# Graph layer with residual norm on one core: the order and the engines of the last split's steps

## The chip, the cores and the metric

One core of one Trainium2 chip runs the kernel. Its time is device microseconds for one execution; the median of 3 runs of the kernel before is 1138.0 us (1137.83 to 1139.56). The profile is of one further execution, whose own numbers stand in a table below. Engines are named as in the profile: PE multiplies matrices and writes PSUM, DVE (VectorE), ACT (ScalarE) and POOL (GpSimd) work element by element, and SP issues most transfers. Each engine works through its own queue in order, so an instruction that waits holds up everything behind it on that engine.

## What is computed

100,000 edges join 6,250 nodes. For each edge the rows of its two nodes and its own row of 128 attributes are multiplied by a 384x128 weight, normalised, scaled and cut at zero. The results are summed by source node, added to the node's own row x, and normalised again:

```
msg_in = jnp.concatenate([x[row], x[col], edge_attr], axis=-1)
h = msg_in @ W + b
h = (h - mu) * jax.lax.rsqrt(var + LN_EPS) * gamma + beta
out = jax.ops.segment_sum(jax.nn.relu(h), row, num_segments=N)
x = _layernorm(x + out, axis=-1)
```

`row` is an edge's source `src`, `col` its target `dst`; edges come sorted by target. The kernel checks the ranges of its inputs and falls back to a general path when they don't fit, which is not run here.

## The kernel before

**Two passes.** Edges come in 782 tiles of 128. The first pass multiplies the attributes and the target rows of four tiles at a time (`edges`, L531 and L535), evicts them (`evict`, L543) and scatters every row to memory, sorted by the block of its source node (`scatters`, L561: one indirect transfer of POOL per tile). There are 50 blocks of 125 nodes. The second pass loads the sorted rows block by block, two blocks (a **pair**) at a time, and needs all scatters of the rows that it loads. The tiles are therefore cut into six **splits** (`SPLITS`): while split s is multiplied and scattered, the pairs of split s-1 are worked through. The last split has 78 tiles, and nothing follows it. Its 25 pairs of 4 tiles, with the finishing of the 50 blocks, are the **tail** (`tail`, L962 to L1001), which starts when the last scatter has landed.

**The steps of a pair** (`class Pair`). `load_pair` (L614, SP) brings the rows `hl`, with the node's number within its block in column D. `ones` (L632, DVE) makes the one-hot matrix `ohe` of all four tiles in one instruction. `turn` (L644, PE) transposes it, `turned` (L648, ACT) copies it to `ohn` as bf16. `pick` multiplies `ohn` with the projected node rows `xa`, twelve matmuls (L671), onto a PSUM bank that was seeded with `hl`. In the tail the seed is a matmul of `hl` with the identity (L665, in `pick`); the banks are called `sel` for even and `hp` for odd pairs. `square` squares and sums the four tiles on ACT (L680) and takes the root (L683), `root` the reciprocal on DVE (L689), `scale` writes the four scaled and cut messages on DVE (L695), `sums` adds them up per node on PE (L704, bank `pa`, of which there is one), and `add` adds that to `acc` on DVE (L712).

**The finishing of two blocks** (`class Finish`). `begin` loads two blocks of x (L725, SP) and forms y from `acc` and x with two instructions of POOL (L728, L729). `stats` adds the shift and the total on DVE (L735, two). `root` squares on ACT (L745, two) and takes a root of its own (L748). `norm` and `moved` (L753, L758, DVE) give scale and shift, `end` applies them with two instructions of POOL (L764, L765; the last two blocks on ACT, L768) and stores (L770, SP).

**The order.** Inside `manual_schedule` PE, DVE, ACT and SP run in the order in which the program calls the steps; POOL's order is left to the scheduler. `work(n)` advances the pairs of the older splits by `FLOW`. Behind the last scatters the old pairs still have steps left. The program calls `tail(-2)` and `tail(-1)`, with the first two one-hots and the first transposition of the last split, between those steps, and then `tail(0)` to `tail(30)`. In `tail(i)` DVE does the reciprocal of pair i-1, the one-hot of i+2, the messages of i-1, the finishing's total of i-3, its reciprocal and shift of i-4, and the addition of i-1; PE does seed and pick of i, the transposition of i+1 and the sums of i-1; ACT does squares and root of finishing i-4, the copy of `ohn` of i+1, squares and root of pair i; POOL has in the built kernel, in turn, L764 and L765 of one block pair and L728 and L729 of the one three later.

Of the kernel before, what the change touches and what calls it, by code (L numbers as in the profile page):

```python
# [50 lines left out]
XG = 4  # L51
ROW = 132
# [31 lines left out]
def fast_path(ctx, tc, io, bad_d):  # L84
# [533 lines left out]
    class Pair:  # L618
# [8 lines left out]
        def ones(self):  # L627

            blk, k = late["blk"], self.k
            self.hl = loaded.pop((self.s, self.p))  # L630
            self.ohe = blk.tile([P, KMAX, P], F32, name="ohe", bufs=4)
            nc.vector.tensor_tensor(self.ohe[:, :k, :],  # L632
                                    self.hl[:, :k, D:D + 1].to_broadcast([P, k, P]),
                                    row_bc(iota_p, k), op=ALU.is_equal)
# [20 lines left out]

        def pick(self, g):
# [3 lines left out]
            if g in self.sel:  # L660
                sel = self.sel[g]
            else:
                name = "hp" if (g + self.p * len(self.groups)) % 2 else "sel"
                sel = psum.tile([P, PT, P], F32, name=name, bufs=BANKS[name])
                nc.tensor.matmul(sel[:, :m, :], ident, self.hl[:, j0:j0 + m, 0:D], start=True,  # L665
                                 stop=False, skip_group_check=True)
                self.sel[g] = sel
            for j in range(m):
                b = 2 * self.p + (j0 + j) % 2
                for i in range(3):  # L670
                    pe(nc.tensor.matmul(sel[:, j, :], self.ohn[:, j0 + j, :],  # L671
                                        xa[:, b, i * D:(i + 1) * D], start=False,
                                        stop=j == m - 1 and i == 2, skip_group_check=True))

# [41 lines left out]
    class Finish:  # L716
# [5 lines left out]
        def begin(self):  # L722
            fin, b0, n = late["fin"], self.b0, self.n
            xs = fin.tile([P, FN, D], F32, name="xs", bufs=3)
            nc.sync.dma_start(flat(xs), io["xblk"][:, b0 * D:(b0 + n) * D])  # L725
            self.y = fin.tile([P, FN, D], F32, name="y", bufs=6)
            engine = nc.gpsimd if b0 + n < NB else nc.vector
            engine.tensor_tensor(self.y, acc[:, b0:b0 + n, 0:D], row_bc(g2, n), op=ALU.mult)  # L728
            engine.tensor_tensor(self.y, self.y, xs, op=ALU.add)  # L729

        def stats(self):
            fin, y = late["fin"], self.y
            total = fin.tile([P, FN], F32, name="total", bufs=4)
            for j in range(self.n):
                nc.vector.scalar_tensor_tensor(y[:, j, :], beta_p, acc[:, self.b0 + j, D:D + 1],  # L735
                                               y[:, j, :], op0=ALU.mult, op1=ALU.add,
                                               accum_out=total[:, j:j + 1])
            self.total = total

        def root(self):  # L740
            fin = late["fin"]
            fsq = fin.tile([P, FN, D], F32, name="fsq")
            var = fin.tile([P, FN], F32, name="var")
# [212 lines left out]
    def at(p):  # L956
        return 0 <= p < n
# [311 lines left out]
```

## Time and profile before

| | us |
|---|---|
| median of 3 runs | 1138.0 |
| the profiled execution's own time | 1138.6 |
| its span, first to last instruction | 1136.7 |
| mean granted clock of PE in it | 0.894 |
| PE, DVE, ACT, POOL busy in the span | 859.8, 882.7, 735.6, 837.0 |
| last scatter issued | 1033.08 |
| first one-hot of the last split starts | 1037.87 |
| first and last pick of the last split start | 1043.09, 1118.72 |
| last write of the result on an engine ends | 1129.76 |

A row of a timeline gives the start, the length, the engine, the line, and in brackets how long the engine stood idle before it and what ended that. "x4" are four instructions shown as one. A length is that of the instruction; the next one of the same engine can start before it is over, so the cost of an instruction on its engine is the distance to the next start.

### The profile page before, as it was taken

The numbers are of one execution on the slowest core, as the hardware profiler recorded it, in microseconds if no ns is written. First come the engines' busy times: TensorE is split into PE (matmuls) and PEld (weight loads), VectorE is DVE, ScalarE is ACT, GpSimd is POOL, SyncE is SP. The second block draws the span as 40 slices with busy tenths as digits, with TensorE's granted clock in tenths as the row PEclk, the third lists the DMA queues.
The fourth block names the chain that finished last, engine by engine and source line by source line (L and its number), as shares of the span: only waits on it lengthen the run. The fifth ranks groups of instructions, "written<-read, shape, count | busy, mean of one in ns | idle before, by whom it ended". The sixth has DMA issues, their size and how long they took to land.

```text
span 1136.7 us, 27306 instructions
## 1 busy us (share of the span) xinstructions
PE 859.8 (76%) x8671; PEld 798.3 (70%) x8671; DVE 882.7 (78%) x2444; ACT 735.6 (65%) x3104; POOL 837.0 (74%) x899
## 2 busy tenths in 40 slices
PE   3657755445877878787778878898989899986994
PEld 2546644345877778686777877888988898975673
DVE  7987776326878777778677778988999987875996
ACT  1334332115666676576766777887988999994996
POOL 2777777777777777777777777777777777773786
PEclk9878786657989989899889999998999999998998
DMA  6799996438877756677777749776877677742562
GB/s 198 230 282 280 292 288 203 140 105 263 252 243 241 246 179 190 216 241 243 226 244 225 229 125 316 253 251 205 279 249 237 209 230 221 237 140 88 159 171 83
DMA packets 126674, 247.47 MB, mean 218 GB/s; under 512 B 47356, under 2 KB 61197, under 8 KB 126519
## 3 DMA queue, kind: packets, MB, share of 16 engines
q1 hardware_dynamic: 100356, 191.52, 56.2%
q0 software_dynamic: 25184, 53.31, 13.2%
q8 instruction: 70, 1.15, 0.4%
q10 hardware_dynamic: 978, 0.80, 0.3%
q14 instruction: 86, 0.70, 0.2%
HBM read 155.74 MB, written 89.80 MB: 216 GB/s over the span
## 4 chain that ended last, share of the span: by engine, by line
PE 29%; DMA 24%; DVE 24%; ACT 11%; issue 7%; POOL 2%; SPq 1%; ACTq 0%; POOLq 0%; DVEq 0%
DMA sorted<-hs,place_i 18%; PE pa L704 9%; DVE msg L695 7%; PE hp L531 7%; PE sel L671 6%; DMA db<-drel_d 4%; ACT sq L680 3%; DVE ohe L632 3%; DVE sc L391 3%; PE beside L428 2%; ACT sel L654 2%; POOL sorted L561 2%; ACT hs L543 2%; ACT ohn L648 2%; PE tr L644 2%
## 5 line engine op out<-in xcount | busy, mean ns | idle before, releaser
L561 POOL DMA_INDIRECT sorted<-hs,place_i x782 | 771.0, 986 | 240.9 <-issue 98.8
L704 PE MATMUL pa<-msg,ohe 128*128 128x130 f32 x1900 | 268.1, 292 | 23.3 <-DVE acc L712 15.3
L531 PE MATMUL hp<-w,eT 128*128 128x128 f32 x1564 | 248.2, 309 | 49.2 <-ACT hs L543 44.3
L543 ACT COPY hs<-hp 128x512 f32<-128x512 f32 x196 | 114.0, 582 | 258.7 <-DMA sorted<-hs,place_i 193.3
L671 PE MATMUL sel<-xa,ohn 128*128 128x128 bf16 x2706 | 198.7, 225 | 106.3 <-ACT sel L654 105.5
L671 PEld LDWEIGHTS <-ohn 128*128 128x128 bf16 x2850 | 182.9, 100 | 133.5 <-issue 112.6
L704 PEld LDWEIGHTS pa<-msg,ohe 128*128 128x128 f32 x1900 | 240.3, 201 | 34.3 <-DVE acc L712 18.7
L695 DVE SCALAR_TENSOR_TENSOR msg<-sel,rstd,cut 128x128 f32<-128x128 f32 x902 | 255.2, 345 | 8.0
L531 PEld LDWEIGHTS hp<-w,eT 128*128 128x128 f32 x1564 | 221.2, 218 | 54.6 <-ACT hs L543 48.8
L680 ACT ACTIVATE sq<-sel 128x128 f32<-128x128 f32 x902 | 238.1, 282 | 17.4 <-PE sel L671 16.7
L680 ACT ACTIVATION_READ_ACCUMULATOR sq<-sel 128x1 f32 x902 | 191.6, 212 | 0.0
L632 DVE TENSOR_TENSOR ohe<-hl,beside 128x1024 f32<-128x1024 f32 (+2 forms) x150 | 147.9, 986 | 37.4 <-DMA hl<-sorted 30.9
L654 ACT COPY sel<-hl 128x512 f32<-128x512 f32 (+1 forms) x225 | 127.9, 568 | 19.4 <-DVE msg L695 19.1
L648 ACT COPY ohn<-tr 128x1024 bf16<-128x1024 bf16 (+2 forms) x150 | 123.7, 825 | 18.4 <-PE tr L644 18.2
L689 DVE RECIPROCAL rstd<-std 128x4 f32<-128x4 f32 (+1 forms) x250 | 42.9, 172 | 84.7 <-ACT std L683 83.8
L519 DVE TENSOR_SCALAR ohd<-db,part_w 128x512 bf16<-128x512 bf16 x194 | 71.8, 370 | 46.7 <-DMA db<-drel_d 25.2
L644 PE MATMUL tr<-ident_h,ohe 128*128 128x128 bf16 x950 | 81.6, 226 | 10.5 <-issue 7.2
L535 PE MATMUL hp<-win,ohd 126*128 126x128 bf16 x782 | 83.3, 233 | 4.1 <-DVE ohd L519 3.5
L683 ACT ACTIVATE std<-ss,eps 128x4 f32<-128x4 f32 (+1 forms) x250 | 74.3, 297 | 8.1
L535 PEld LDWEIGHTS <-ohd 126*128 126x128 bf16 x782 | 66.9, 106 | 8.7 <-DVE ohd L519 3.7
L712 DVE TENSOR_TENSOR acc<-acc,pa 128x260 f32<-128x260 f32 x125 | 52.3, 418 | 26.4 <-PE pa L704 26.3
L644 PEld LDWEIGHTS <-ohe 128*128 128x128 bf16 x950 | 63.8, 102 | 11.8 <-issue 7.7
(159 smaller groups left out, 807.6 us busy)
## 6 DMA issues: line engine op xcount, KB each, us to landing
eT<-in_eT SPq DMA_DIRECT2D x96, 512.0 KB
hl<-sorted SPq DMA_DIRECT2D x75, 528.0 KB
db<-drel_d SPq DMA_DIRECT2D x96, 256.0 KB
sorted<-empty SPq DMA_DIRECT2D x100, 198.0 KB
hl<-sorted SPq DMA_DIRECT2D x50, 264.0 KB
sorted<-hs,place_i POOLq DMA_INDIRECT x782
hl<-sorted SPq DMA_DIRECT2D x25, 396.0 KB
sorted<-empty SPq DMA_DIRECT2D x50, 132.0 KB
```

The costliest lines, as they stand in the source:

```text
L531: pe(nc.tensor.matmul(hp[:, j, :], eT[:, at], w[:, 2, :], start=j == 0, stop=False, skip_group_check=True), 4)
L535: pe(nc.tensor.matmul(hp[:, j, :], oh[:3 * WN, at], win[:3 * WN, :], start=False, stop=j == m - 1, skip_group_check=True))
L543: nc.scalar.copy(hs[:, :m, 0:D], hp[:, :m, :])
L561: i = nc.gpsimd.indirect_dma_start(out=sorted_d[s][:, :], out_offset=bass.IndirectOffsetOnAxis(ap=place_i[:parts, t:t + 1], axis=0), in_=h ...
L632: nc.vector.tensor_tensor(self.ohe[:, :k, :], self.hl[:, :k, D:D + 1].to_broadcast([P, k, P]), row_bc(iota_p, k), op=ALU.is_equal)
L644: pe(nc.tensor.transpose(tr[:, j, :], half[:, j0 + j, 1::2], ident_h))
L648: nc.scalar.copy(self.ohn[:, :self.k, :], self.tr[:, :self.k, :])
L654: nc.scalar.copy(self.sel[g][:, :m, :], self.hl[:, j0:j0 + m, 0:D])
L671: pe(nc.tensor.matmul(sel[:, j, :], self.ohn[:, j0 + j, :], xa[:, b, i * D:(i + 1) * D], start=False, stop=j == m - 1 and i == 2, skip_gro ...
L680: nc.scalar.activation(sq[:, j, :], self.sel[g][:, j, :], AF.Square, accum_out=ss[:, j:j + 1])
L695: nc.vector.scalar_tensor_tensor(self.msg[:, j0 + j, 0:D], self.sel[g][:, j, :], rstd[:, j:j + 1], cut, op0=ALU.mult, op1=ALU.max)
L704: pe(nc.tensor.matmul(self.pa[:, h, :], self.ohe[:, j, :], self.msg[:, j, :], start=(j == h), stop=(j == k - 2 + h)), 4)
```

## The change

It concerns the last split alone. All steps of the old pairs are called before its first one-hot; 14 matmuls of ones, each into the single `tr` bank, follow them on PE. From the third pair on POOL makes the one-hots, tile by tile, four instructions per pair. The seed of odd pairs is a copy by DVE, that of even pairs stays a matmul, called one step earlier. The sums of squares of pair i and of finishing i-3 lie in one tile, with one root on ACT and one reciprocal on DVE for both. The finishing of block pair i-2 begins in step i (before: i-1) and has one step less between its parts. `end` is one instruction per block with both scale and shift, on POOL; for the last two block pairs one block is done by ACT and one by DVE. x is loaded in the step before the pair's pick, with five buffers in place of three. Four pairs are loaded at the start in place of two, and each later one in the step after its buffer's last reader is called.

In the built kernel POOL's order in the steady part is: the four one-hots of pair i+2, the two of `end` of i-4, the two of `begin` of i-2. Each of the 14 matmuls of ones waits on PE's own semaphore for the one before it, except the first.

```
+WARM = 14
-        def ones(self):
+        def ones(self, on_pool=False):
...
+            if on_pool:
+                for j in range(k):
+                    nc.gpsimd.tensor_scalar(self.ohe[:, j, :], iota_row, self.hl[:, j, D:D + 1],
+                                            None, op0=ALU.is_equal)
+            else:
...
+        def begin_pick(self, by_pe):
+            m = self.k
+            name = "hp" if self.p % 2 else "sel"
+            sel = psum.tile([P, PT, P], F32, name=name, bufs=BANKS[name])
+            if by_pe:
+                nc.tensor.matmul(sel[:, :m, :], ident, self.hl[:, :m, 0:D], start=True,
+                                 stop=False, skip_group_check=True)
+            else:
+                nc.vector.tensor_copy(sel[:, :m, :], self.hl[:, :m, 0:D])
+            self.sel[0] = sel
...
+        def squares(self, ss):
+            sq = late["blk"].tile([P, PT, P], F32, name="sq")
+            for j in range(self.k):
+                nc.scalar.activation(sq[:, j, :], self.sel[0][:, j, :], AF.Square,
+                                     scale=float(D), accum_out=ss[:, j:j + 1])
...
+        def load(self):
+            self.xs = late["fin"].tile([P, FN, D], F32, name="xs", bufs=5)
+            nc.sync.dma_start(flat(self.xs), io["xblk"][:, self.b0 * D:(self.b0 + self.n) * D])
...
+        def end(self, engines):
             y, n = self.y, self.n
+            for j in range(n):
+                engine = engines[j % len(engines)]
+                if engine is nc.scalar:
                     nc.scalar.activation(y[:, j, :], y[:, j, :], AF.Identity,
                                          bias=self.shift[:, j:j + 1], scale=self.rstd[:, j:j + 1])
+                else:
+                    engine.tensor_scalar(y[:, j, :], y[:, j, :], self.rstd[:, j:j + 1],
+                                         self.shift[:, j:j + 1], op0=ALU.mult, op1=ALU.add)
...
+    def ones_at(p):
+        if at(p):
+            x[p].ones(on_pool=p > 1)
+
+    def roots(i):
+        lo, hi = 0 if at(i) else kp, kp + FN if at(i - 3) else kp
...
+        nc.scalar.activation(std[:, lo:hi], sums_of.pop(i)[:, lo:hi], AF.Sqrt, bias=eps,
+                             scale=1.0 / D ** 3)
+        rstd_of[i] = std, lo, hi
+
+    def reciprocals(i):
...
+        nc.vector.reciprocal(rstd[:, lo:hi], std[:, lo:hi])
+        if at(i):
+            x[i].rstd[0] = rstd
+        if at(i - 3):
+            f[i - 3].moved(rstd[:, kp:kp + FN])
 
     def tail(i):
+        if i == -1:
+            x[0].begin_pick(True)
+        if at(i):
+            x[i].pick(0)
+        if at(i + 1):
+            x[i + 1].turn()
+        reciprocals(i - 1)
+        if at(i - 2):
+            x[i - 2].add()
+            f[i - 2].begin(nc.gpsimd if i - 2 < n - 1 else nc.vector)
+        if at(i + 2):
+            ones_at(i + 2)
+            load_next()
+        if at(i - 1):
+            x[i - 1].scale(0)
+        if at(i + 1):
+            if i >= 0:
+                x[i + 1].begin_pick((i + 1) % 2 == 0)
+            f[i + 1].load()
+        if at(i - 2):
+            f[i - 2].stats()
+        if at(i) or at(i - 3):
+            sums_of[i] = late["blk"].tile([P, kp + FN], F32, name="tsums", bufs=3)
+        if at(i - 3):
+            f[i - 3].square(sums_of[i][:, kp:])
+        if at(i):
+            x[i].squares(sums_of[i])
+        roots(i)
+        if at(i + 1):
             x[i + 1].turned()
+        if at(i - 1):
             x[i - 1].sums()
+        if at(i - 4):
+            f[i - 4].end([nc.gpsimd] if i - 4 < n - 2 else [nc.scalar, nc.vector])
+            f[i - 4].store()
...
-    for p in range(2):
-        load_pair(s, p)
-    work(n_last - 8 - n_steps)
-    tail(-2)
-    work(n_last - 4 - n_steps)
-    tail(-1)
-    work(n_last - n_steps)
+    for p in range(4):
+        load_next()
+    work(n_last + 1 - n_steps)
+    for p in range(WARM):
+        tr = psum.tile([P, PT, P], F32, name="tr", bufs=BANKS["tr"])
+        nc.tensor.matmul(flat(tr), ones_h, row_bc(ones_h, PT), start=True, stop=True)
     nc.vector.tensor_copy(beta_p, beta2)
...
-    for i in range(n + 6):
+    ones_at(0)
+    for i in range(-1, n + 4):
         tail(i)
```

113 lines of the change are left out of this document (35 added, 78 removed).

## The prediction

> **What bounds the kernel now.** The first line of the page gives the span. The profiled execution took 1138.6 us, 1.9 more than its span and 0.6 more than the median; the sum below is made against 1138.6 and its difference taken off 1138.0.
>
> ```profile
> span 1136.7 us, 27306 instructions
> ```
>
> The change touches only what follows the last scatter, so I read the timeline from there. The rows below are its start.
>
> ```profile
> 1032.20 1.13 DVE L695 SCALAR_TENSOR_TENSOR msg<-sel,rstd,cut 128x128 f32<-128x128 f32 x4
> 1033.08 0.87 POOL L561 DMA_INDIRECT sorted<-hs,place_i  x1 [0.30 <-issue]
> 1035.24 10.43 SPq L614 DMA_DIRECT2D hl<-sorted  x6
> 1037.87 0.69 DVE L632 TENSOR_TENSOR ohe<-hl,beside 128x512 f32<-128x512 f32 x1 [4.55 <-DMA hl<-sorted]
> ...
> 1038.95 2.10 PE L704 MATMUL pa<-msg,ohe 128*128 128x130 f32 x8 [6.45 <-DVE acc L712]
> ...
> 1041.27 2.02 PE L665 MATMUL sel<-hl,ident 128*128 128x512 f32 x2
> ...
> 1043.09 1.09 PE L671 MATMUL sel<-xa,ohn 128*128 128x128 bf16 x12
> ```
> ```profile
> 1038.00:1042.00 4.00, 3.05 (x13) 2.70 (x14) 2.37 (x6) 0.48 (x1) 0.00 (x0) 0.50 0.38 143
> ...
> 1060.00:1080.00 20.00, 19.15 (x162) 14.17 (x163) 18.76 (x85) 18.73 (x97) 16.28 (x26) 1.00 0.63 170
> ```
>
> The last scatter is issued at 1033.08, the load of its rows at 1035.24, and DVE waits 4.55 us for them in front of the first one-hot. The addition of an old pair stands behind that one-hot, so PE idles 6.45 us "<-DVE acc" and sums the last old pair only from 1038.95. It does so slowly: between 1038 and 1042 the granted clock is 0.50 of full speed, against 1.00 later, and the seed takes 2.02 us there. The first pick starts at 1043.09.
>
> Then comes the steady part; rows of the chain of work that ended last, and of the timeline:
>
> ```profile
> 1059.22 0.57 DVE ohe L632
> ...
> 1061.56 0.86 PE sel L665 x2
> ...
> 1065.52 0.57 DVE ohe L632
> ```
> ```profile
> 1059.38 0.68 POOL L728 TENSOR_TENSOR y<-acc,g 128x256 f32<-128x256 f32 x1
> ...
> 1059.71 1.12 DVE L695 SCALAR_TENSOR_TENSOR msg<-sel,rstd,cut 128x128 f32<-128x128 f32 x4
> ...
> 1060.01 0.57 ACT L648 COPY ohn<-tr 128x512 bf16<-128x512 bf16 x1
> 1060.14 0.73 POOL L729 TENSOR_TENSOR y<-y,xs 128x256 f32<-128x256 f32 x1
> ...
> 1060.20 1.36 PE L704 MATMUL pa<-msg,ohe 128*128 128x130 f32 x8 [0.30 <-DVE msg L695]
> 1060.48 0.28 ACT L680 ACTIVATE sq<-hp 128x128 f32<-128x128 f32 x1
> ...
> 1060.75 0.34 DVE L735 SCALAR_TENSOR_TENSOR y<-beside,acc,y 128x128 f32<-128x128 f32 x1
> ...
> 1061.28 0.16 DVE L753 RECIPROCAL frstd<-fstd 128x2 f32<-128x2 f32 x1
> ...
> 1061.48 0.16 DVE L758 SCALAR_TENSOR_TENSOR shift<-total,frstd 128x2 f32<-128x2 f32 x1
> 1061.52 0.61 POOL L764 TENSOR_TENSOR y<-y,frstd 128x256 f32<-128x256 f32 x1 [0.66 <-DVE frstd L753]
> 1061.60 0.42 DVE L712 TENSOR_TENSOR acc<-acc,pa 128x260 f32<-128x260 f32 x1
> 1061.66 0.30 ACT L683 ACTIVATE std<-ss,eps 128x4 f32<-128x4 f32 x1
> ...
> 1061.86 0.39 ACT L745 ACTIVATE fsq<-y,total 128x128 f32<-128x128 f32 x1
> 1061.99 0.18 DVE L689 RECIPROCAL rstd<-std 128x4 f32<-128x4 f32 x1
> 1062.09 0.66 DVE L632 TENSOR_TENSOR ohe<-hl,beside 128x512 f32<-128x512 f32 x1
> ...
> 1062.26 0.83 PE L671 MATMUL sel<-xa,ohn 128*128 128x128 bf16 x12
> ...
> 1062.76 0.29 ACT L748 ACTIVATE fstd<-var,eps 128x2 f32<-128x2 f32 x1
> ...
> 1062.93 0.39 PE L644 MATMUL tr<-ident_h,ohe 128*128 128x128 bf16 x4
> ```
> ```profile
> 1118.72 0.83 PE L671 MATMUL sel<-xa,ohn 128*128 128x128 bf16 x12
> ...
> 1128.88 0.88 ACT L768 ACTIVATE y<-y,shift,frstd 128x128 f32<-128x128 f32 x2 [0.71 <-DVE shift L758]
> ```
>
> The chain comes back to the same one-hot after 6.30 us (1059.22 to 1065.52), for two pairs. From the first pick (1043.09) to the 25th (1118.72) are 24 steps in 75.63 us: **3.15 us per pair**. Distances between starts say what a pair costs on each engine. DVE: reciprocal 0.10, one-hot 0.57, messages 1.04, totals 0.53, reciprocal and shift 0.20 and 0.12, addition 0.39: 2.95 us. ACT: copy 0.47, squares 1.18, root 0.20, two squares 0.90, second root at least 0.20: 2.95. PE: sums 1.36 less an overlap, seed 0.86, pick 0.67, transposition 0.27: about 3.1 with waits. POOL: 0.76 and 0.73 for `begin`, twice 0.61 and a hop for `end`: 2.8. So three engines are nearly full, and the rest of the 3.15 is waits between them. The end lasts 11.04 us, from the 25th pick to the last write at 1129.76; what follows it (stores, flag) stays.
>
> **The change part by part.**
>
> *Start.* Two rows more, of the last old sums at full clock and of matmuls of ones in an earlier stage (shortest, median and longest of three):
>
> ```profile
> 1031.34 1.16 PE L704 MATMUL pa<-msg,ohe 128*128 128x130 f32 x8 [0.90 <-DVE acc L712]
> ```
> ```profile
> L588 PE MATMUL sel<-ones_h x3: 380/467/634, 217.0 to 217.7; 128*128 128x512 bf16 x3
> ```
>
> DVE's last old messages end at 1033.33. Without the one-hot in front, the addition takes 0.42, PE's last old sums 1.16: they end at 1034.9. This takes the stall of 6.45 us away, but the new split cannot begin before its rows at 1037.87, which stay where they are, as does the load at 1035.24 behind the scatter. What is late next are the 14 matmuls of ones. They share one bank, and each waits for the one before it to end, so their spacing is their whole length plus a hop. The same shape took 0.380 us at best and 0.634 at worst; POOL's own wait between 1059.38 + 0.68 and 1060.14 cost 0.08, so I take 0.38 + 0.06 = 0.44. Fourteen are 6.2 us: PE is free at 1041.1 (0.38 each: 1040.2; 0.634 each: 1043.8). Behind them on PE's queue stand the seed (0.86), the transposition (0.39) and, after ACT's copy (0.59), the first pick: 1041.1 + 0.86 + 0.39 + 0.59 + 0.1 for hops = 1043.0. That is 0.1 ahead of 1043.09. The fillers keep the clock up, which saves about 2 us of slow matmuls, and cost about as much by ending 2.5 us behind the first one-hot (1038.6). Ends: 1.0 gained to 2.6 lost.
>
> Which end it is hangs on the clock. The row at 1031.34 kept 1.16 us after 0.90 us of idling, and the row of 1038 to 1042 has 0.50 after 6.45 us of it; the last old sums will have idled 1.2 us (1032.5 to 1033.75). The Trainium skill ("TensorE: Matmul & The Clock Gate", Part 1) says that the clock falls to half only after an idle window of about 3.4 us. Both rows agree with it; by that rule the fillers run at 0.38 each, while at 0.634 the whole sum below would be 1.7 in place of 4.4.
>
> *Steady part, taken away or moved.* DVE loses the one-hot (0.57) and one reciprocal (0.10), and gains 0.57 in every second pair for the seed; I price a 128x512 copy like the one-hot of that size. DVE: 2.28 us in even, 2.85 in odd steps. PE loses half its seeds (0.43 per pair): about 2.6. ACT loses a root: 2.75. Taking these alone, one would say 0.3 us per pair. But two circles form. First, ACT now copies `ohn` of the next pair behind the squares of this one, and the next pick waits for it: pick 0.83, squares 1.18, root 0.20, copy 0.59, two hops: 2.9. Second, DVE now waits in each step for POOL: shift, addition 0.12 + 0.42 and a hop, `begin` on POOL 0.76 + 0.73 and a hop, totals 0.53, reciprocal 0.20, shift: 2.85, and 2.92 when POOL does the two instructions of `end` in between, after the shift. Behind that waiting total on DVE stand the reciprocal, addition and messages of the next pair, for which PE's sums wait. So the floor is 2.9, not 2.6. Before, the fullest sum was 2.95 and the step 3.15; with half that surcharge I take **3.0 us per pair** (ends 2.9 and 3.1). 24 steps gain 24 x 0.15 = 3.6 us.
>
> *POOL's part* has no row, and decides whether that holds. Six tile instructions of 128x128 come (four one-hots, two of `end`), two of 128x256 go.
>
> ```profile
> 0.84 0.23 POOL L154 IOTA iota_i<- 128x128 int32 x1 [0.40 <-POOLq L1260]
> ...
> 2.29 0.28 POOL masks.py:199 TENSOR_SCALAR_AFFINE_SELECT ident<-ident 128x128 f32<-128x128 f32 x1
> 2.53 0.10 POOL L197 MEMSET empty<- 128x8 f32 x1
> ```
>
> An iota of that size is 0.23 us long; a compare-and-select that reads one such tile is 0.28 long and lets the next start after 0.24. Half of L764 (two inputs, 128x256) is 0.31. The bounds are 0.15 (iota less the same overlap) and 0.35; I take 0.22, beside the compare, its nearest kin. POOL: 6 x 0.22 + 1.49 = 2.8, hidden under the circles. It is hidden up to 0.25.
>
> The Trainium skill ("GPSIMD Engine Reference", section 3.1) puts a one-input body at 1.03 cycles per element, which gives as an estimate 0.11 us for 128 elements plus dispatch, and section 7 charges about 102 cycles for each small read that doesn't overlap. If the per-partition scalar is such a read, 0.09 us would come on top of my 0.22, which is the first rival at 0.31; no row here shows it.
>
> *x ahead, loads ahead.* One group row says what it can give:
>
> ```profile
> L729 POOL TENSOR_TENSOR y<-y,xs 128x256 f32<-128x256 f32 x19 | 13.8, 728 | 4.5 <-DMA xs<-in_xblk 3.4
> ```
>
> POOL waited 3.4 us in all for x, beside other engines' work. Stores now stand behind the loads of rows and x on SP; each issue is short, and nothing waits for a store until the end. I count it at nothing in the steady part (if rows came late: a step's delay, about 3 us once).
>
> *End.* From the 25th pick: about one step to the reciprocal of pair 24 (3.2), one to the next (2.95), shift, addition and `begin` on DVE 1.4, totals 0.7, squares 0.9, root 0.3, reciprocal and shift 0.4, the write 0.45 with both blocks side by side: 10.3. Gain 0.7.
>
> **Sum:** 0.1 + 3.6 + 0.7 = 4.4 us: 1134.2 for the profiled execution, **1133.6 us** as a median.
>
> **Rivals.**
>
> *POOL becomes the bound (slower).* In POOL's steady order the one-hots stand ahead of `begin`, for which DVE waits. At a us per tile instruction a step is 6a + 1.49. It passes 3.15 at 0.277, and eats the 0.8 us of start and end too at 0.282. At 0.31 (half of L764) it is 3.35: 24 x 0.20 - 0.8 = +4.0, 1142.0 us; at 0.35, 3.59 and +9.8, 1147.8. For: POOL takes 0.61 us for 256 elements where DVE takes 0.42 for 260 (L764, L712), and the new instructions read a scalar per partition. Against: its one-input rows (0.23, 0.28).
>
> *Nothing to speak of.* The circles hold at 3.1 and the fillers end at 1042.5: -1.4 + 1.2 + 0.7 = 0.5 gained, 1137.5. For: in before, too, the step was 0.2 above the fullest engine. Against: the stall of each second step in the chain is on instructions that leave.
>
> *More than forecast.* Tile instructions at 0.15 to 0.2, a step of 2.9, and fillers at 0.38: 1.0 + 6.0 + 0.7 = 7.7, 1130.3. For: both circles come out at 2.9 by rows. Against: they are coupled, and odd steps of DVE are 2.85 by themselves.
>
> **How the numbers follow.** Forecast (gain 2.5 to 6): 0.50. More: 0.16. Nothing to speak of: 0.12. POOL bound: 0.22, of which half ends under 1141.5. The range 1129.5 to 1141.5 leaves out that half and about half of "more", 0.19 in all. A measurement of this kernel can tell about 0.2% (2.3 us) from no change. Faster by more than that: 0.50 + 0.16 = 0.66; within: 0.12; slower: 0.22.
>
> **What would show it.** In the profile after: picks 3.0 us apart, and the first at about 1043.0; matmuls of ones 0.44 apart, ending at 1041; one-hots on POOL 0.22 apart; DVE's totals waiting on POOL's second instruction of `begin`, not on ACT. It is wrong if POOL has no idle time between 1060 and 1110 (then the first rival), if PE picks the first pair before 1041 (fillers cheaper than their waits), or if DVE waits for loaded rows.

## The result and the profile after

The changed kernel takes **1163.45 us** (median of 6 runs, 1161.23 to 1164.58) against 1138.33 us (6 runs, 1137.08 to 1139.56) for the kernel before on the same chip: a ratio of 1.0225, interval 1.0211 to 1.0238. The forecast was 1133.6 us with a range to 1141.5. It is slower, on the side of the first rival and beyond that rival's highest price. The profiled execution took 1164.58 us; its page begins:

```profile
span 1162.8 us, 27348 instructions
```

The timeline around the start of the last split answers to the first rows of the prediction (rows in between are left out at "..."):

```profile
1027.24 0.87 POOL L562 DMA_INDIRECT sorted<-hs,place_i  x1 [0.30 <-issue]
...
1031.53 1.16 PE L720 MATMUL pa<-msg,ohe 128*128 128x130 f32 x8 [1.21 <-DVE acc L728]
...
1032.52 5.99 PE L1051 MATMUL tr<-ones_h 128*128 128x512 bf16 x14
...
1033.39 1.29 DVE L638 TENSOR_TENSOR ohe<-hl,beside 128x512 f32<-128x512 f32 x2
...
1038.35 1.02 PE L667 MATMUL sel<-hl,ident 128*128 128x512 f32 x2
...
1040.27 0.84 PE L681 MATMUL sel<-xa,ohn 128*128 128x128 bf16 x12 [0.68 <-ACT ohn L654]
```

The first one-hots are there at 1034.1, but PE multiplies ones until 1038.3, and the first pick starts at 1040.27. The last scatter has moved, too, from 1033.08 to 1027.24, which nothing in the prediction provides for. POOL's rows of one step, later on, then the last pick and the last write on ACT:

```profile
1084.41 0.68 POOL L745 TENSOR_TENSOR y<-acc,g 128x256 f32<-128x256 f32 x1
1085.17 0.72 POOL L746 TENSOR_TENSOR y<-y,xs 128x256 f32<-128x256 f32 x1
1085.88 2.33 POOL L635 TENSOR_SCALAR ohe<-iota_row,hl 128x128 f32<-128x128 f32 x4
1088.20 0.87 POOL L776 TENSOR_SCALAR y<-y,trstd,shift 128x128 f32<-128x128 f32 x2
1089.03 0.68 POOL L745 TENSOR_TENSOR y<-acc,g 128x256 f32<-128x256 f32 x1
```
```profile
1144.51 0.84 PE L681 MATMUL sel<-xa,ohn 128*128 128x128 bf16 x12
```
```profile
1155.70 1.02 ACT L773 ACTIVATE y<-y,shift,trstd 128x128 f32<-128x128 f32 x2
```

Read the distances between POOL's starts: 0.76, 0.71, 2.32, 0.83, with no gap, and then the same again: **4.62 us per pair**. The waits between 1048 and 1145 name the victim, DVE's total behind the second instruction of `begin` (us in total, times, longest):

```profile
DVE y L752 <- POOL y L746: 42.6, 22, 2.3
```

The busy times by stretch of 20 us (length, PE, PEld, which is PE's loading of weights, DVE, ACT, POOL, granted clock, DMA share, GB/s) show who has no time left. Before, PE, DVE and ACT stood near 19 and POOL at 16.3; now POOL is at 19.6 to 19.7, and PE, DVE and ACT are at 10 to 14:

```profile
1080.00:1100.00 20.00, 13.69 (x116) 10.53 (x114) 10.48 (x47) 10.68 (x56) 19.61 (x35) 0.91 0.44 132
1100.00:1120.00 20.00, 12.89 (x101) 9.47 (x101) 11.76 (x56) 12.03 (x65) 19.69 (x36) 0.91 0.35 109
```

The account of the two spans, by the last scatter, the first pick and the 25th:

| us | before | after | difference |
|---|---|---|---|
| last scatter issued | 1033.08 | 1027.24 | -5.84 |
| from there to the first pick | 10.01 | 13.03 | +3.02 |
| 24 steps | 75.63 | 104.24 | +28.61 |
| 25th pick to the end of the span | 17.98 | 18.29 | +0.31 |
| span | 1136.7 | 1162.8 | +26.10 |

### The profile page after: what moved, and what is told of

The parts are those of the page before. It is cut to its first block, busy times and chain, and to the rows that moved or that the text cites. A ratio compares the mean times of both kernels' runs of the same rounds, so it can differ in the third digit from the quotient of the medians.

```text
span 1162.8 us, 27348 instructions
## 1 busy us (share of the span) xinstructions
PE 868.9 (75%) x8661; PEld 804.2 (69%) x8661; DVE 873.1 (75%) x2413; ACT 727.6 (63%) x3082; POOL 872.8 (75%) x989
## 5 line engine op out<-in xcount | busy, mean ns | idle before, releaser
L562 POOL DMA_INDIRECT sorted<-hs,place_i x782 | 763.0, 976 | 243.4 <-issue 104.9
L720 PE MATMUL pa<-msg,ohe 128*128 128x130 f32 x1900 | 272.5, 295 | 41.5 <-DVE msg L711 31.1
L720 PEld LDWEIGHTS pa<-msg,ohe 128*128 128x128 f32 x1900 | 245.0, 204 | 61.3 <-issue 37.4
L711 DVE SCALAR_TENSOR_TENSOR msg<-sel,rstd,cut 128x128 f32<-128x128 f32 x850 | 240.7, 345 | 7.9
L696 ACT ACTIVATE sq<-sel 128x128 f32<-128x128 f32 x850 | 223.5, 281 | 20.8 <-PE sel L681 20.5
L696 ACT ACTIVATION_READ_ACCUMULATOR sq<-sel 128x1 f32 x850 | 180.1, 212 | 0.0
L638 DVE TENSOR_TENSOR ohe<-hl,beside 128x1024 f32<-128x1024 f32 (+2 forms) x127 | 132.9, 1047 | 35.9 <-DMA hl<-sorted 28.0
L705 DVE RECIPROCAL rstd<-std 128x4 f32<-128x4 f32 (+1 forms) x225 | 38.5, 171 | 76.4 <-ACT std L699 73.7
L650 PE MATMUL tr<-ident_h,ohe 128*128 128x128 bf16 x950 | 81.6, 226 | 10.3 <-issue 7.4
L699 ACT ACTIVATE std<-ss,eps 128x4 f32<-128x4 f32 (+1 forms) x225 | 66.9, 297 | 7.3
```

Of the source, the lines that this page charges most:

```text
L562: i = nc.gpsimd.indirect_dma_start(out=sorted_d[s][:, :], out_offset=bass.IndirectOffsetOnAxis(ap=place_i[:parts, t:t + 1], axis=0), in_=h ...
L638: nc.vector.tensor_tensor(self.ohe[:, :k, :], self.hl[:, :k, D:D + 1].to_broadcast([P, k, P]), row_bc(iota_p, k), op=ALU.is_equal)
L650: pe(nc.tensor.transpose(tr[:, j, :], half[:, j0 + j, 1::2], ident_h))
L696: nc.scalar.activation(sq[:, j, :], self.sel[g][:, j, :], AF.Square, accum_out=ss[:, j:j + 1])
L711: nc.vector.scalar_tensor_tensor(self.msg[:, j0 + j, 0:D], self.sel[g][:, j, :], rstd[:, j:j + 1], cut, op0=ALU.mult, op1=ALU.max)
L720: pe(nc.tensor.matmul(self.pa[:, h, :], self.ohe[:, j, :], self.msg[:, j, :], start=(j == h), stop=(j == k - 2 + h)), 4)
```

## The experiments

The experiments ran on seven chips, and six of them took 1350 to 1369 us for the kernel before; there the granted clock is lower in the middle stages (0.80 to 0.84 between 300 and 600 us and 0.86 to 0.89 between 600 and 900, against 0.90 to 0.91 and 0.95 to 0.96), and the part ahead of the last scatter lasts some 210 to 240 us longer. The tail of the old order costs the same there (24 steps 75.6 to 76.2 us in six traces, against 75.6), so steps are compared in us, and ratios always with the kernel before on the same chip. "Step" below is the mean distance of picks once the pipeline is full. Theory A at first was that POOL's amount alone makes the loss; theory B that something else in the new order does so as well. The code shown is shortened.

**POOL's one-hots back on DVE.**

```diff
-            x[p].ones(on_pool=p > 1)
+            x[p].ones(on_pool=False)
```


> The changed kernel with one part undone: DVE makes all one-hots again, everything else stays. Theory A (POOL's amount of work): in the changed kernel a one-hot tile costs POOL 0.58 us and an end tile 0.435, so a step is 4 x 0.58 + 2 x 0.435 + 0.76 + 0.71 = 4.66 us. Without the one-hots POOL needs 2.34, DVE 2.57 + 0.57 = 3.14; the step falls to about 3.2 and the time by 24 x 1.4 = 34 us, to about 1130. Theory B (the new order: DVE's totals wait in each step for POOL's begin, a circle that exists whoever makes the one-hots): the step stays at 4 us or more, the time above 1148.

Measured: 1383.52 us against 1368.01, ratio 1.0109 (1.0069 to 1.0149); step 3.48. So taking all one-hots off POOL brings the step from 4.62 to 3.48, neither to A's 3.2 nor to B's 4: the loss has a second part. The time missed by more than the step, as the first pick came 18.41 us behind the last scatter here (13.03 in the result); the matmuls of ones took 8.96 us, of which more below. POOL isn't full: it is busy for 12.67 us of 20. The rows of one round:

```profile
1322.24 0.88 POOL L776 TENSOR_SCALAR y<-y,trstd,shift 128x128 f32<-128x128 f32 x2 [1.14 <-DVE shift L765]
...
1323.09 0.69 POOL L745 TENSOR_TENSOR y<-acc,g 128x256 f32<-128x256 f32 x1
...
1323.85 0.72 POOL L746 TENSOR_TENSOR y<-y,xs 128x256 f32<-128x256 f32 x1
...
1324.61 0.35 DVE L752 SCALAR_TENSOR_TENSOR y<-beside,acc,y 128x128 f32<-128x128 f32 x1 [0.58 <-POOL y L746]
```

It is the prediction's second circle: the shift (1321.90), `end` (0.34 later, 0.85 to the next start), `begin` (0.76 and 0.76), totals (0.55), reciprocal (0.22), and the next shift at 1325.38: 3.48. `end` waits for the shift, and `begin`, which needs only the addition (over at 1322.40), stands behind it.

**Which form costs POOL what.** The kernel leaves the four one-hots out and has four other instructions on the same tiles:

```diff
+ tensor_scalar(ohe[:, 0], iota_row, 64.0, None, op0=is_equal)
+ tensor_scalar(ohe[:, 1], iota_row, hl[:, 1, D:D+1], None, op0=subtract)
+ tensor_scalar(ohe[:, 2], iota_row, 0.5, None, op0=mult)
+ tensor_tensor(ohe[:, 3], iota_row, hl[:, 3, D:D+1].to_broadcast([P, P]), op=subtract)
```


> The changed kernel, but the four tile instructions of POOL per pair are four other forms, so the one-hots are left out: tile 0 compares with a constant, tile 1 subtracts the per-partition scalar, tile 2 multiplies by a constant, tile 3 subtracts with two tensor inputs. Theory A1 (comparing is what costs): tile 0 takes 0.58 us, tile 1 0.3 or less. Theory A2 (the per-partition scalar costs): tile 0 takes 0.3 or less, tile 1 0.5 or more. Theory A3 (a dispatch of about 0.3 that every such instruction pays): all of tiles 0 to 2 above 0.4. Tile 3 by half of the 128x256 rows: 0.35.

```profile
1321.12 0.53 POOL L635 TENSOR_SCALAR ohe<-iota_row 128x128 f32<-128x128 f32 x1
1321.64 0.61 POOL L636 TENSOR_SCALAR ohe<-iota_row,hl 128x128 f32<-128x128 f32 x1
1322.21 0.54 POOL L638 TENSOR_SCALAR ohe<-iota_row 128x128 f32<-128x128 f32 x1
1322.71 0.40 POOL L639 TENSOR_TENSOR ohe<-iota_row,hl 128x128 f32<-128x128 f32 x1
1323.10 0.89 POOL L780 TENSOR_SCALAR y<-y,trstd,shift 128x128 f32<-128x128 f32 x2
```

1395.94 us in one run against 1368.01; step 4.29, again the sum of POOL's distances. By distance to the next start: compare with a constant 0.52, subtract a scalar per partition 0.57, multiply by a constant 0.50, two inputs 0.39. So neither the comparison nor the scalar is what costs (the scalar about 0.05 to 0.07): every instruction of this form is more than twice what I took. That is the sign of the third theory; that a dispatch is the reason is not shown.

Nor is it work of DVE at the same time that makes them slow. In the changed kernel the first eight one-hots run on POOL while DVE stands idle, from 1035.28 to 1042.65:

```profile
1035.54 4.67 POOL L635 TENSOR_SCALAR ohe<-iota_row,hl 128x128 f32<-128x128 f32 x8 [7.43 <-PE tr L1051]
```
```profile
1042.65 0.18 DVE L990 RECIPROCAL trstd<-tstd 128x4 f32<-128x4 f32 x1 [7.37 <-ACT tstd L981]
```

Eight in 4.67 us are 0.58 each, as beside a working DVE. The two tiles of `end`, with two operations each, are cheaper (0.43). I then guessed that one operation is the slow case:

```diff
+ tensor_scalar(ohe[:, 0], iota_row, hl[:, 0, D:D+1], 1.0, op0=is_equal, op1=mult)
+ tensor_scalar(ohe[:, 1], iota_row, hl[:, 1, D:D+1], hl[:, 1, D:D+1], op0=mult, op1=add)
+ tensor_scalar(ohe[:, 2], iota_row, 64.0, 1.0, op0=is_equal, op1=mult)
+ tensor_copy(ohe[:, 3], iota_row)
```


> POOL's four one-hots are left out, and instructions of other forms stand in their place: compare with the scalar of each partition and multiply by 1; multiply and add with two scalars of each partition; compare with a constant and multiply by 1; copy. Theory A, that one operation costs POOL more than two (0.58 and 0.52 against 0.435 for the `end` tile): 0.43 to 0.48 for each of the first three. Rival, that the compare or the reading of another tile costs it: 0.52 to 0.62 for the first and third, and the second tells whether writing another tile than is read matters (0.435 if not). The copy: below 0.40 by both.

```profile
1338.77 0.72 POOL L635 TENSOR_SCALAR ohe<-iota_row,hl 128x128 f32<-128x128 f32 x1
1339.46 0.46 POOL L637 TENSOR_SCALAR ohe<-iota_row,hl 128x128 f32<-128x128 f32 x1
1339.89 0.64 POOL L639 TENSOR_SCALAR ohe<-iota_row 128x128 f32<-128x128 f32 x1
1340.48 0.28 POOL L641 COPY ohe<-iota_row 128x128 f32<-128x128 f32 x1
```

That guess falls: compare and multiply takes 0.69 with the scalar of each partition and 0.59 with constants, more than the comparison alone (0.58 and 0.52). Multiply and add takes 0.43, into another tile as well as in place; of the pairs tried it alone is cheap. A copy takes 0.27, near the rows that I had gone by. (1404.9 us in one run against 1369.06.)

**Half of the one-hots on each engine.** Two tiles of four on POOL, two in one instruction of DVE.

```diff
-                for j in range(k):
+                for j in range(2):
...
+                nc.vector.tensor_tensor(self.ohe[:, 2:k, :],
...
```


> The changed kernel with two of the four one-hot tiles of a pair on POOL and two on DVE. Theory A: POOL 2 x 0.58 + 0.87 + 1.47 = 3.50 us per step, about 1.15 less than the changed kernel, 24 x 1.15 = 28 us: about 1136. Theory B: no proportion to the number of tiles; the step stays at 4 or more, the time above 1148.

1384.68 against 1368.01, ratio 1.0107 (1.0056 to 1.0158); step 3.50, as theory A has it. Its time, a little less than that of the kernel before, is missed: the first pick came 18.41 behind the last scatter here, too. POOL's distances are 1.16 for two one-hots, 0.84, 0.77 and 0.74: 3.51, no gap. That the step is the same as with none on POOL is chance: here POOL is full, there it is the circle.

**The old steps first, in the kernel before.** `tail(-2)` and `tail(-1)` called behind the last old step, nothing else.

```diff
-    work(n_last - 8 - n_steps)
-    tail(-2)
-    work(n_last - 4 - n_steps)
-    tail(-1)
-    work(n_last - n_steps)
+    work(n_last + 1 - n_steps)
     nc.vector.tensor_copy(beta_p, beta2)
+    tail(-2)
+    tail(-1)
```


> The kernel before with one part alone: all steps of the old pairs ahead of the last split's first one-hots, no matmuls of ones, nothing else. If the stall in front of the last old sums and the half clock behind it cost what the profile of before shows (2.1, 2.0 and 1.1 us for sums, seed and first pick), the first pick comes 2 us sooner and the time falls by about 2, to 1136. If the rows' arrival alone sets the start, nothing changes: 1138.

1367.3 against 1368.01, ratio 0.9993 (0.9972 to 1.0014): nothing. The last scatter is at 1260.89 and the first pick at 1271.46, 10.57 later. (In the kernel before it is 10.01; in the old order on chips like this one, in traces of further experiments below, 10.38 to 11.35.) The one-hot no longer stands ahead of the old steps, but the last old sums end 6.9 us behind the last scatter (1267.80), and the first one-hot follows the last addition at 1268.50. What stood behind the stall was no later than this.

**The changed kernel beside two of its variants.** First itself, then `begin` of a pair ahead of `end` of an older one on POOL (all one-hots on DVE), then the changed kernel without its matmuls of ones.

> The changed kernel unaltered, beside the others on this chip. Both theories: a step of 4.62 us (POOL's sum: four one-hots of 0.583, two tiles of the end of 0.435, 0.76 and 0.71) and 22 to 28 us more than the kernel before on the same chip.

1385.78 against 1350.81, ratio 1.0257 (1.0220 to 1.0294); step 4.62 as expected, last scatter to first pick 13.58. The loss of 35 us is above the 22 to 28 expected: on this chip the last scatter, at 1247.61, gave nothing back.

```diff
-            x[p].ones(on_pool=p > 1)
+            x[p].ones(on_pool=False)
...
+    pools = ExitStack()
+    pools.enter_context(tc.manual_schedule(engines={mybir.EngineType.Pool}))
...
+    pools.close()
```


> All one-hots on DVE, and on POOL `begin` of a pair ahead of `end` of an older one. Theory A, that the step of 3.48 us with all one-hots on DVE is the circle totals, reciprocal, shift, `end`, `begin`, totals (0.55 + 0.22 + 0.34 + 0.85 + 0.76 + 0.76 by the rows of that run): without `end` in the circle the step falls to DVE's own sum, 3.1 to 3.2 us, so 7 to 9 us less than with the order of before the swap, 2 to 8 us above the kernel before. Theory B, that the new order has a floor of its own near 3.5 us on ACT and PE (the one-hots' copy behind the squares, the pick behind it): the step stays at 3.4 to 3.5.

1351.24 against 1350.81, ratio 1.0007 (0.9986 to 1.0029), so better than the 2 to 8 us of loss expected; step **3.135** (2.96 and 3.31 by turns), 24 steps 73.96. With POOL in the program's order, `begin` comes ahead of the next `end` and waits only for the addition:

```profile
1299.58 0.88 POOL L776 TENSOR_SCALAR y<-y,trstd,shift 128x128 f32<-128x128 f32 x2
1301.50 0.69 POOL L745 TENSOR_TENSOR y<-acc,g 128x256 f32<-128x256 f32 x1 [1.04 <-DVE acc L728]
```

The circle is the second part of the loss, and theory B's floor of 3.4 to 3.5 on ACT and PE is not there. DVE is now full: 19.79 us busy of 20. The first pick comes 12.81 behind the last scatter.

```diff
-WARM = 14
+WARM = 0
```


> The changed kernel without its 14 matmuls of ones. Theory A, that they hold the first pick back: from the last scatter to the first pick 9 to 11 us in place of 13.0, and 2 to 5 us less than the changed kernel on the same chip. Theory B, that they pay for themselves through the clock: the granted clock falls to a half behind the old sums, the first picks come as late as before, and the time is the same within 1.5 us. Both: a step of 4.62 us.

1380.63 us, 5.2 less than the changed kernel on the same chip (2 to 5 expected); against the kernel before 1.0233 (1.0195 to 1.0271), an interval that overlaps the other's. The trace tells more: the last scatter is at 1246.59 and the first pick, the last of these rows, at 1255.01:

```profile
1251.33 1.16 PE L720 MATMUL pa<-msg,ohe 128*128 128x130 f32 x8 [1.66 <-DVE acc L728]
...
1253.94 0.40 PE L650 MATMUL tr<-ident_h,ohe 128*128 128x128 bf16 x4 [0.42 <-DVE ohe L638]
1255.01 0.84 PE L681 MATMUL sel<-xa,ohn 128*128 128x128 bf16 x12 [0.68 <-ACT ohn L654]
```

8.42 later in place of 13.58, with steps of 4.62 as expected. The matmuls of ones held the split back by 5 us and bought nothing here: the last old sums in the first row (1.16 us for eight) and the transposition (0.40 for four) are as fast as at full clock without them.

**Towards a faster version.** One one-hot tile of four on POOL, `begin` ahead of `end`, three matmuls of ones.

```diff
-WARM = 14
+WARM = 3
...
-                for j in range(k):
...
+                nc.gpsimd.tensor_scalar(self.ohe[:, k - 1, :], iota_row, self.hl[:, k - 1, D:D + 1],
...
+                nc.vector.tensor_tensor(self.ohe[:, :k - 1, :],
...
```


> Of each pair's four one-hots one on POOL and three on DVE, `begin` ahead of `end` on POOL, 3 matmuls of ones in place of 14. Theory A: POOL's sum 1.49 + 0.87 + 0.58 = 2.94, DVE's 3.13 - 0.14 = 2.99, no circle above 2.9: a step of 3.0 to 3.15 us, the first pick 9 us behind the last scatter; 0 to 5 us less than the kernel before. Theory B: a step near 3.45 and 5 to 9 us more than the kernel before.

1347.86 against 1350.81, ratio 0.9982 (0.9963 to 1.0002); step 3.135, first pick 8.74 behind the last scatter. Theory A's bounds hold, but the tile on POOL did not shorten the step against the swap alone: DVE's sum is 2.99 here by the expectation, and what holds the step at 3.135 stays open. Next, DVE seeds only each fourth pair, and no matmuls of ones:

```diff
-WARM = 3
+WARM = 0
...
-                x[i + 1].begin_pick((i + 1) % 2 == 0)
+                x[i + 1].begin_pick((i + 1) % 4 != 3)
```


> As the version with one of four one-hots on POOL and `begin` ahead of `end`, but no matmuls of ones, and DVE seeds each fourth pair in place of each second. Theory A, that DVE's sum sets the step there (19.4 us busy of 20, a step of 3.13): DVE loses 0.16 per pair and PE gains 0.22, so a step of 3.0 to 3.05 and 1.5 to 3 us less than that version, 3 to 7 us less than the kernel before. Rival, that a circle over ACT holds 3.1: a step of 3.1 to 3.15, and at most 1 us less than that version, from the start alone.

1362.95 against 1369.06, ratio 0.9962 (0.9943 to 0.9981); step 3.03, as expected, and the first pick 9.17 behind the last scatter. Here the last old sums took 1.69 us and the two matmuls of the seed 1.92, where 1.16 and 1.02 are the times at full clock: without matmuls of ones the clock can be low at this place. The same with three of them:

> As the version with DVE seeding each fourth pair, with 3 matmuls of ones in place of none. In the version without them the second last and last old sums took 1.16 and 1.69 us and the seeds 1.92, so the clock was not whole there. If the three hold the clock, the first pick comes 8.5 to 9 us behind the last scatter and the time is 0 to 1 us less than without them; if the clock falls ahead of them, they cost 3 x 0.64 = 1.9 us. Both: a step of 3.03 and 3 to 7 us less than the kernel before.

1125.72 against 1139.21, ratio **0.9872** (0.9853 to 0.9892), on a chip like that of the result; the step is 3.03. The three matmuls did not hold the clock, which had fallen ahead of them (granted clock 0.50 between 1029.5 and 1032):

```profile
1027.16 1.16 PE L722 MATMUL pa<-msg,ohe 128*128 128x130 f32 x8 [0.90 <-DVE acc L730]
1029.53 2.10 PE L722 MATMUL pa<-msg,ohe 128*128 128x130 f32 x8 [1.21 <-DVE acc L730]
1031.42 1.70 PE L1053 MATMUL tr<-ones_h 128*128 128x512 bf16 x3
```

The seed behind them is fast again (1.02), but the first pick comes 9.66 behind the last scatter, not the 8.5 to 9 of the better case. The gain in time is far more than expected, so the kernel before was profiled there, too:

> The kernel before, for its profile on this chip. If only what precedes the last scatter depends on the chip, the steps are 3.15 us here too, and from the last scatter to the end of the span it is 103.6 us within 1; if the tail depends on the chip as well, it is longer by the ratio of the whole times.

Its 24 steps take 3.17 us each, and from the last scatter to the end it is 103.95 us, both as expected and as on the first chip. The first pick and the 25th of the faster version, and then of the kernel before on that chip:

```profile
1034.89 0.84 PE L683 MATMUL sel<-xa,ohn 128*128 128x128 bf16 x12 [0.68 <-ACT ohn L656]
...
1106.56 0.84 PE L683 MATMUL sel<-xa,ohn 128*128 128x128 bf16 x12
```
```profile
1045.40 0.85 PE L671 MATMUL sel<-xa,ohn 128*128 128x128 bf16 x6
...
1121.55 0.83 PE L671 MATMUL sel<-xa,ohn 128*128 128x128 bf16 x12
```

| us | before | faster version | difference |
|---|---|---|---|
| last scatter issued | 1035.15 | 1025.23 | -9.92 |
| to the first pick | 10.25 | 9.66 | -0.59 |
| 24 steps | 76.15 | 71.67 | -4.48 |
| 25th pick to the end of the span | 17.55 | 17.14 | -0.41 |

The tail gains 5.5 us, about what was expected. The rest comes from ahead of it. (These are single executions; the last scatter of the kernel before, 1035.15 here, was at 1033.08 in its other trace.)

**Why the last scatter comes sooner.** POOL's instructions up to the last scatter are the same ones in the kernel before, the changed one and the versions with `begin` ahead of `end`. The scatters' lengths (shortest, median, longest in ns, then the first and last start), of the kernel before and the changed one:

```profile
L561 POOL DMA_INDIRECT sorted<-hs,place_i x782: 868/967/2044, 23.5 to 1033.1; - x196
```
```profile
L562 POOL DMA_INDIRECT sorted<-hs,place_i x782: 870/958/2039, 23.8 to 1027.2; - x196
```

The median is 958 to 961 in the nine traces so far of kernels in which POOL makes one-hots or the instructions in their place, which all hold a comparison, and 967 to 971 in the five that had none. The mean over all 782 is 986 before and 976 after; 782 x 10 ns are 7.8 us. Theory C: a comparison on POOL anywhere in the program makes the scatters cheaper from the start. Three kernels add one instruction to the kernel before, in the one-hots of the last pair, into a tile that nobody reads: a comparison on POOL, a memset on POOL, a comparison on DVE.

```diff
+            if self.s == n_split - 1 and self.p == NB // 2 - 1:
+                scr = blk.tile([P, P], F32, name="scr", bufs=1)
+                nc.gpsimd.tensor_scalar(scr, iota_row, self.hl[:, 0, D:D + 1], None, op0=ALU.is_equal)
```


> The kernel before with one more instruction, in the last pair's one-hots: POOL compares one tile of 128x128 with a scalar of each partition into a tile that nobody reads. Theory C, that a program in which POOL compares has cheaper scatters from the start (median 958 to 961 ns in the eight kernels with such or like instructions, 967 to 971 in the four without): the scatters take 958 ns here too and the last one comes 6 to 9 us sooner, so 5 to 9 us less where the scatters set the pace. Rival, that the scatters differ for some other reason (places in memory, the number of instructions): 967 ns and the time of before within 1.5 us.

> As the last, but the one instruction more is a memset by POOL. If any instruction more of POOL shifts the scatters, 958 ns; by theory C 967 ns and the time of before within 1.5 us.

> As the first of the three, but DVE makes the comparison. By theory C 967 ns and the time of before within 1.5 us; if the tile more and its place in memory shift the scatters, 958 ns.

The comparison on POOL, the memset, the comparison on DVE:

```profile
L561 POOL DMA_INDIRECT sorted<-hs,place_i x782: 871/958/2073, 23.4 to 1248.7; - x196
```
```profile
L561 POOL DMA_INDIRECT sorted<-hs,place_i x782: 871/971/2016, 23.7 to 1248.5; - x196
```
```profile
L561 POOL DMA_INDIRECT sorted<-hs,place_i x782: 866/967/1828, 23.3 to 1243.8; - x196
```

958 against 971 and 967: the lengths go as theory C says. (The comparison runs at 1326.9 us, behind all scatters; the memset, which waits for nothing, runs at 276.0.) The times do not answer: on this chip the scatters leave POOL more room (it is busy for 189 us of the 300 between 300 and 600, against 229 in the kernel before on the first chip), and the shorter ones did not bring the last one forward. The ratios are 1.0039 (1.0013 to 1.0066), 1.0013 (0.9995 to 1.0031) and 1.0007 (0.9986 to 1.0027), so the first is even a little slower. The comparison was run on two more chips, the second time beside the version with the swap alone, in which POOL compares nothing:

> The kernel before with the one comparison on POOL in the last pair, once more. Where scatters set the pace (the kernel before near 1139 us), the last scatter comes 6 to 9 us sooner than in the kernel before, and the time is 3 to 8 us less; if cheaper scatters are taken up by other waits, the time is that of before within 2 us. Where something else sets the pace (the kernel before near 1350), 958 ns and no gain, as in its first run.

> The kernel before with the one comparison on POOL, a third time. Where scatters set the pace (the kernel before near 1139 us): the last scatter 6 to 9 us sooner and 3 to 8 us less; if other waits take it up, the time of before within 2 us. Where they do not (near 1350): 958 to 962 ns and no gain, as twice before.

> All one-hots on DVE, `begin` of a pair ahead of `end` of an older one: a kernel of the new order in which POOL compares nothing. Where scatters set the pace: by theory C scatters of 967 to 971 ns, the last one as late as in the kernel before, and the time of before within 2 us; if the rest of the change makes the scatters cheaper, 5 to 9 us less. Where they do not, the time of before within 3 us, as in its first run.

Both chips were again of the kind on which the kernel before takes 1350 us and more. The scatters took 962 and 962 ns with the comparison and 967 without; the ratios are 1.0021 (1.0003 to 1.0039), 1.0003 (0.9981 to 1.0024) and 1.0020 (1.0000 to 1.0039). That cheaper scatters make the last one come 6 to 10 us sooner is thus not shown by the one comparison alone. It rests on the two pairs of traces where the kernel before takes 1138 to 1139 us (changed kernel and before, faster version and before), and these kernels differ in more than the comparison.

The third of these has the same code as the swap above and shows what 14 matmuls of ones can cost. There they took 5.99 us; here, much as in the two versions above whose first pick came 18.41 behind the last scatter:

```profile
1263.16 1.26 PE L720 MATMUL pa<-msg,ohe 128*128 128x130 f32 x8 [2.12 <-DVE acc L728]
1264.94 2.10 PE L720 MATMUL pa<-msg,ohe 128*128 128x130 f32 x8 [0.52 <-DVE acc L728]
1266.83 8.95 PE L1051 MATMUL tr<-ones_h 128*128 128x512 bf16 x14
```

The clock has fallen ahead of them (granted 0.79 between 1263 and 1264.9, then 0.50), each takes 0.64, and the first pick comes 18.40 behind the last scatter in place of 12.81. By the medians this run is 4.6 us above the kernel before, where 3 were expected at most.

## Why the prediction was wrong

**Steady part: the step that failed is "POOL's part".** It took a = 0.22 us per tile instruction, with bounds of 0.15 and 0.35, and so hid POOL's sum of 2.8 under a step of 3.0. Measured are 0.58 for a one-hot and 0.43 for a tile of `end`, and the 24 steps took 104.24 us in place of 72. Both prices lie above the upper bound, because the bounds came from POOL instructions of other kinds: an iota, a compare-and-select by index, and half of a two-input instruction. (The lower bound was also reckoned wrongly: 0.23 less the overlap of 0.04 is 0.19; and no row is named for 0.35.) The nearest form for one input, the copy, does take 0.27; compare, subtract and multiply with a scalar take twice that. The rule of the rival itself was right: with the measured prices its sum 4 x 0.58 + 2 x 0.43 + 1.49 is 4.67 (step 4.62), and the test that the prediction named for it, POOL without idle time, is what the profile shows. Totals waiting for `begin`, which it named as a sign of the forecast, came true as well, though in the forecast the wait was to fit into 3.0 us.

In the Trainium skill, "GPSIMD Engine Reference", section 3.1, one-input bodies run at 1.03 cycles per element, an estimate of 0.11 us here, to which the dispatch comes. The forms tried took 0.27 to 0.69; no run varies the width of a tile, so how much of that is dispatch stays open. The charge for a small read in section 7 of the same page of the Trainium skill, 0.09 us as an estimate, is above the 0.05 to 0.07 that the scalar per partition costs; that this scalar is such a read is not shown.

**The circles.** The second circle was put at 2.92 with `end` between shift and `begin`. It exists, and sets the step when POOL has room; with `end` at its real price and the hop of 0.34 it is 3.48. Without `end` in it the step was 3.135, which is DVE's own sum (2.28 and 2.85 by turns, and 0.57 for the one-hots: 3.14 in the mean); with half of DVE's seeds moved back to PE it was 3.03, near the forecast of 3.0. So no floor of ACT or PE above 3.03 was met; that DVE's sum sets the step is shown for the swap alone, as the version with one tile on POOL had a smaller sum and the same step.

**Start.** The forecast of the first pick, 9.9 us behind the last scatter, was 3.1 too short. The spacing of the matmuls of ones was right (0.43 for 0.44). What failed is the place where they begin. The old sums were to end 1.8 us behind the last scatter, and ended 5.45 behind it (1032.69): the scatters had become quicker and the old steps hardly so (their last messages ended at 1031.15, 2.2 sooner, where the scatters were 5.8 sooner). So the chain of old sums and matmuls, which the prediction too had whole on the path, began 3.6 us later as seen from the scatter. The first pick at 1040.27 is ahead of 1041, which the prediction named as a sign of being wrong; but the reason it gave, cheaper fillers, is not the cause.

The bound for a low clock, 0.634 each, was also met, on other chips. The Trainium skill, "TensorE: Matmul & The Clock Gate", Part 1, was read as "half clock only after an idle window of about 3.4 us", and this case disagrees with that reading. In the changed kernel, PE's last two idle stretches ahead of the matmuls of ones, 0.90 and 1.21 us, left the old sums behind each at 1.16; in the faster version the sums behind the same two stretches took 1.16 and 2.10, and no stretch in the 9 us ahead is longer. So the length of an idle stretch does not settle it. The same Part 1 of the Trainium skill also says that the window runs freely. That would let the same stretches end one way or the other, and these two traces agree with it.

**End.** 10.3 us from the 25th pick to the last write were forecast; the changed kernel took 12.2 (1144.51 to 1156.72). There the circle with `end` ahead of `begin` still runs twice behind the last pick (shifts at 1145.60, 1149.06 and 1152.50, 3.45 apart). The faster version, without that circle (2.86 apart), took 10.45 (1106.56 to 1117.01).

**x ahead** was counted at nothing. No wait for x is left in front of POOL between 1048 and 1145; what that is worth by itself no run shows.

**What the prediction left out**: that the stage ahead of the last split could change. It gave back 5.8 of the 31.9 us that the tail lost. That was luck, and not enough of it to change the verdict.

## What to carry to other kernels

Where an instruction moves to an engine on which the trace shows none of its form, the nearest rows bound it badly: the highest bound was 0.35 and the price 0.58. If the forecast turns over at 0.28, that is a reason for an even chance, not for 0.22. An engine that is filled up also needs its order looked at: here the two instructions of `end` ahead of `begin` cost 0.35 us per pair with POOL a third idle. And matmuls that are to keep a clock up belong where PE idles anyway; behind the last work ahead of a stage they are that stage's delay, here 5 us.

## What was not expected of the hardware

- POOL on a 128x128 f32 tile, by distance of starts: copy 0.27, two inputs with a broadcast column 0.39, multiply and add 0.43, one multiply 0.50, one compare with a constant 0.52, subtract a scalar per partition 0.57, compare with one 0.58, compare and multiply 0.59 and 0.69. Multiply and add is cheaper than one multiply. The one added comparison of the kernel before took 0.62 us on POOL and 0.28 on DVE.
- A comparison on POOL at the end of a program goes with shorter indirect transfers ahead of it: medians over all 782 of 958 to 962 ns in twelve traces with one or more, 967 to 971 in eight without. By what means stays open.
- The same 14 matmuls of 128x512 took 5.99 or 8.95 us in different runs of one kernel, and idle stretches of the same length left the clock whole in one kernel and at a half in another.
